# Four layers of attention and experts on one Trainium2 core: square roots and a sigmoid moved from ScalarE to VectorE

## The chip, the core and the metric

The kernel runs on one core of a Trainium2 chip. A core has five engines that run their own queues of instructions: TensorE (PE in the profile; PEld is its loading of weights), VectorE (DVE), ScalarE (ACT), GpSimd (POOL) and SyncE (SP). They meet in semaphores: an instruction waits in its queue until what it needs is there, and everything behind it in the queue waits too. ScalarE evaluates functions such as Exp, Silu or Sqrt from tables; before a function whose table is not the loaded one, its queue holds an ACT_TABLE_LOAD. Time is the device time of one execution in microseconds (us). The measured number is the median of several runs; one more run is recorded by the profiler and read in detail.

## What is computed

Activations `x` (4 sequences of 512 tokens, 256 features) pass through four layers. Each layer normalizes `x`, adds a cross attention to a context of 64 rows a sequence, normalizes again, and adds a feed-forward part:

```python
x = x + _L0_xattn_ref(_layernorm(x), ctx_1024, ...)     # softmax attention, 16 heads
x = x + _L0_ffn_ref(_layernorm(x), ...)                 # 8 experts, 2 for each token
x = x + _L1_xattn_ref(ctx_1024, ctx_1024, _layernorm(x), ...)  # exponential features
x = x + _L1_ffn_ref(_layernorm(x), ...)                 # latent attention, then 7 experts
x = x + _L2_xattn_ref(_layernorm(x), ctx_1024)          # nearest context row by cosine
x = x + _L2_ffn_ref(_layernorm(x), ...)                 # FP4 quantized feed-forward
x = x + _L3_xattn_ref(_layernorm(x), ctx_1024, ctx_1024, ...)
x = x + _L3_ffn_ref(_layernorm(x), ...)                 # 8 experts, 2 for each token
```

The change touches the roots and the sigmoid in these formulas:

```python
def _layernorm(x, axis=-1, eps=1e-05):
    m = jnp.mean(x, axis=axis, keepdims=True)
    v = jnp.var(x, axis=axis, keepdims=True)
    return (x - m) / jnp.sqrt(v + eps)
...
def rmsnorm(x, w):                                      # layer 1, twice
    norm = jnp.sqrt(jnp.mean(x * x, axis=-1, keepdims=True)) + EPS
    return x / norm * w
...
probs = jax.nn.sigmoid(logits)                          # layer 1, the router
...
def _l2norm(x):                                         # layer 2, tokens and context
    n = jnp.linalg.norm(x, axis=-1, keepdims=True)
    return x / jnp.maximum(n, EPS)
```

## The kernel before

The 2048 tokens lie in 16 tiles of 128 rows that stay in SBUF; four tiles (512 tokens, one sequence) are a group. Every stage is a loop over the four groups, written as Python generators whose steps are taken in turn, so that the next group's norm and queries fall between the current group's products. A framework then orders the instructions of each engine by its own estimate, except where the program fixes the order: on TensorE in the cross attentions and in the latent attention, on VectorE and SyncE in the three routed expert stages.

*Layer norm* (`layernorm_steps`, L336 to L345): four pairs of statistics on VectorE into `ln_mv`, a square root of four columns on ScalarE (`ln_sd`, L339), then on VectorE a reciprocal (`ln_rs`, L342) and the shift (`ln_sh`, L343), then four normalizations on ScalarE (`xn`, `xl` or `l2xn`, L345). Every stage begins with one for each group.

*Cross attentions* (layers 0, 1, 3; three stretches of the profile): the scores of a group come in two halves of four PSUM banks (`ps_cx`, L557 and L561) and there is one buffer for them. ScalarE's exponential (`cpr`, L563) must have read the first half before TensorE can write the second. The next group's norm and the routing norm of the group before are in ScalarE's queue in the same stretch. Then come the sums (`crs`, L581), the values (`ps_cy`, `ps_p`) and the residual addition (`x`, L615).

*Routed experts* (layers 0, 1, 3): blocks of 128 rows are fetched, transposed (`ps_xe`, `e_xT`), multiplied with the gate and up weights (`ps_gu`, L1044), passed through Silu on ScalarE (`e_s`, L1060) and a product on VectorE (`e_h`, L1061), transposed (`ps_he`, `e_hT`), multiplied with the down weights (`ps_de`, L1086), weighted (`e_y`, L1088) and scattered by GpSimd (L1089). The routing of the last group and the first results run between the blocks.

*Latent attention* (layer 1): `mla_heads` makes a layer norm (`xl`), an RMS norm (sum of squares on ScalarE at L354, square root `rms_n` at L362, `rms_e` at L364, `rms_r` at L366, scaling `xn` on VectorE at L368), and the heads. In the loop TensorE makes scores (`ps_ms`, L1283), VectorE takes the row maxima (`mq`, L1288), TensorE makes the transposed scores (`ps_mx`, L1298), ScalarE the exponential (`mpr`, L1300), GpSimd the mask (L1302), TensorE the sums (`ps_mo`, L1321). After each group a second RMS norm and the router follow (`mla_after`), with the sigmoid at L1380. Before its loop GpSimd clears the tiles of the heads (L1401 to L1408).

*Layer 2*: the context's norm (`l2_context`, L1519), then for each group a layer norm, a sum of squares and the length of each token (L1545 to L1548), the similarities (`ps_sim`, `sim` at L1557) and the chosen row; then another layer norm, and for each tile the FP4 quantization (`f_am` to `f_y`, L1584 to L1612 on VectorE, the last product on GpSimd, L1613), the products (`ps_f`, L1731), Silu (`fs`, L1741), the second quantization and the down product (`ps_fd`, L1753).

## Time and profile before

| what | us |
|---|---|
| median of 3 runs | 1979.29 |
| lowest and highest of them | 1974.59, 1983.53 |
| the profiled execution | 1971.78 |
| its span | 1970.1 |
| mean granted clock of TensorE in it | 0.933 |

| stretch of the span | what runs | span, us | TensorE busy | VectorE busy | ScalarE busy |
|---|---|---|---|---|---|
| 0 to 166 | cross attention 0 | 166 | 121.9 | 88.1 | 59.5 |
| 166 to 543 | experts 0 | 377 | 361.3 | 179.7 | 101.6 |
| 543 to 695 | cross attention 1 | 152 | 129.5 | 66.4 | 61.8 |
| 695 to 1175 | latent attention | 480 | 420.0 | 220.7 | 189.6 |
| 1175 to 1375 | experts 1, start of layer 2 | 200 | 163.7 | 109.9 | 74.7 |
| 1375 to 1560 | layer 2, FP4 | 185 | 166.7 | 158.3 | 85.5 |
| 1560 to 1700 | cross attention 3 | 140 | 110.2 | 77.9 | 50.7 |
| 1700 to 1970 | experts 3 and the end | 270 | 240.4 | 106.8 | 61.0 |

The busy times are those of the profile's stretches, added where two or three of them make one row. A row of a group of instructions is read like this: line, engine, operation, what it writes and reads, how many, then busy time and mean ns of one, then the idle time of the engine just before them and what ended it. The chain that ended last goes back from the last instruction to what released it at each step; a piece of it has its start, its length, and engine, tile and line. "Issue" is time in which the engine waited for nothing that the profile shows.

### The profile page before, as it was taken

Reading aid. Unit: us, or ns where it says so; the run is one execution under the profiler, and the core shown is the slowest. Engines: PE = TensorE matmul, PEld = TensorE weight load, DVE = VectorE, ACT = ScalarE, POOL = GpSimd, SP = SyncE. Lnnn points to the kernel's source line nnn. Section 1 sums busy time; section 2 is a strip of 40 time slices with the busy share of each in tenths; the row PEclk is TensorE's granted clock in tenths of the full one; section 3 lists DMA queues with packets and bytes.
Section 4 is the critical chain, followed back from the end, with each engine's and each line's share of the span. In section 5 each row is a group of like instructions: output and inputs, shape, how many; then the busy total and the mean of one; then the engine's idle time right before and its main releaser. Section 6 shows DMA issues by size and latency. Waiting matters only on the chain.

```text
span 1970.1 us, 25945 instructions
## 1 busy us (share of the span) xinstructions
PE 1713.7 (87%) x8752; PEld 972.3 (49%) x8752; DVE 1007.7 (51%) x2979; ACT 684.3 (35%) x1265; POOL 448.9 (23%) x626
## 2 busy tenths in 40 slices
PE   5878999999979878898999888887898887899995
PEld 2435666666645333343443344444565544455553
DVE  3655544445444444444455535546899556553332
ACT  3343222223244232335344433234455343322221
POOL 2031211123230021122122222233313102221133
PEclk7988999999979978998999998998999889899998
DMA  9629778878300000000002034873000001679885
GB/s 277 183 77 339 253 288 285 293 286 307 131 25 1 17 24 1 1 1 22 1 5 64 12 106 155 293 261 104 13 1 1 12 1 36 235 268 318 298 321 199
DMA packets 109349, 271.61 MB, mean 138 GB/s; under 512 B 13408, under 2 KB 71200, under 8 KB 99104
## 3 DMA queue, kind: packets, MB, share of 16 engines
q1 hardware_dynamic: 87648, 232.42, 35.0%
q0 software_dynamic: 10176, 28.00, 3.7%
q10 hardware_dynamic: 11392, 9.53, 1.5%
q8 instruction: 70, 1.15, 0.2%
q14 instruction: 63, 0.52, 0.1%
HBM read 220.48 MB, written 49.42 MB: 137 GB/s over the span
## 4 chain that ended last, share of the span: by engine, by line
PE 68%; DVE 17%; ACT 7%; issue 3%; POOL 2%; DMA 2%; ACTq 0%; SPq 0%; DVEq 0%; POOLq 0%
PE ps_gu L1044 20%; PE ps_de L1086 9%; PE ps_ms L1283 4%; PE ps_mo L1321 3%; PE ps_p L612 2%; DVE mq L1288 2%; PE ps_f L1731 2%; PE ps_mx L1298 2%; PE ps_bc L591 2%; PE ps_he L1073 2%; PE ps_xT L377 2%; ACT cpr L563 2%; PE ps_cx L557 1%; PE ps_cy L597 1%; ACT xn L345 1%
## 5 line engine op out<-in xcount | busy, mean ns | idle before, releaser
L1044 PE MATMUL ps_gu<-e_wgu,e_xT 128*128 128x352 f32 (+1 forms) x1088 | 429.3, 535 | 21.7 <-DVE e_xT L1036 14.6
L1044 PEld LDWEIGHTS ps_gu<-e_wgu,e_xT 128*128 128x128 f32 x1088 | 198.0, 193 | 164.2 <-issue 70.3
L1086 PE MATMUL ps_de<-e_wd,e_hT 128*128 128x256 f32 x932 | 239.0, 394 | 10.8 <-ACT e_hT L303 4.8
L1086 PEld LDWEIGHTS ps_de<-e_wd,e_hT 128*128 128x128 f32 x932 | 175.7, 194 | 84.5 <-issue 39.0
L1061 DVE TENSOR_TENSOR e_h<-e_s,ps_gu 128x352 f32<-128x352 f32 (+2 forms) x155 | 83.3, 537 | 253.5 <-PE ps_gu L1044 183.8
L1089 POOL DMA_INDIRECT ys<-e_y,e_to x116 | 114.1, 984 | 422.1 <-ACT e_y L1088 282.3
L1288 DVE TENSOR_REDUCE mq<-ps_ms 128x2 f32<-128x256 f32 (+3 forms) x128 | 105.7, 825 | 136.3 <-PE ps_ms L1286 136.1
L1060 ACT ACTIVATE e_s<-ps_gu 128x352 f32<-128x352 f32 (+2 forms) x155 | 74.1, 478 | 267.9 <-PE ps_gu L1044 261.7
L1088 ACT ACTIVATE e_y<-ps_de,e_wt 128x256 f32<-128x256 f32 x116 | 55.0, 474 | 258.2 <-PE ps_de L1086 251.0
L1300 ACT ACTIVATE mpr<-ps_mx 128x1024 f32<-128x1024 f32 (+3 forms) x128 | 90.1, 704 | 146.5 <-PE ps_mx L1298 143.6
L1283 PE MATMUL ps_ms<-mkT,mqT 32*128 32x512 f32 (+3 forms) x512 | 111.5, 514 | 23.6 <-DVE mq L1288 22.4
L873 POOL DMA_INDIRECT xs<-xn,e_at x96 | 94.6, 986 | 118.7 <-DVE e_fi L907 37.8
L1302 POOL TENSOR_SCALAR_AFFINE_SELECT mpr<-mpr 128x256 f32<-128x256 f32 x128 | 52.1, 410 | 245.1 <-ACT mpr L1300 245.0
L1298 PE MATMUL ps_mx<-mqm,mkT 32*128 32x128 f32 (+3 forms) x512 | 106.9, 494 | 0.9 <-ACT mpr L1300 0.9
L1321 PE MATMUL ps_mo<-mpr,va 128*32 128x128 f32 (+3 forms) x512 | 96.4, 458 | 4.5 <-POOL mpr L1302 4.5
L1073 PE MATMUL ps_he<-consts_sb,e_h 128*128 128x128 f32 x466 | 76.6, 277 | 16.4 <-DVE e_h L1061 13.7
L1167 POOL TENSOR_TENSOR x<-x,e_r 128x256 f32<-128x256 f32 x90 | 66.7, 751 | 84.5 <-DMA e_r<-ys 81.0
L1731 PE MATMUL ps_f<-w,xqT 128*128 128x352 f32 x256 | 84.5, 471 | 0.9 <-ACT xqT L1699 0.9
L557 PE MATMUL ps_cx<-q,kbd 32*128 32x512 f32 x256 | 45.8, 818 | 44.0 <-ACT cpr L563 44.0
L1283 PEld LDWEIGHTS ps_ms<-mkT,mqT 32*128 32x128 f32 x512 | 40.7, 194 | 78.7 <-DVE mq L1288 54.2
L1033 DVE COPY e_xT<-ps_xe 128x256 f32<-128x256 f32 x78 | 32.9, 422 | 80.6 <-PE ps_xe L1030 80.6
L1073 PEld LDWEIGHTS ps_he<-consts_sb,e_h 128*128 128x128 f32 x466 | 54.0, 139 | 38.7 <-DVE e_h L1061 23.7
(317 smaller groups left out, 2814.7 us busy)
## 6 DMA issues: line engine op xcount, KB each, us to landing
e_wgu<-in_e0gu SPq DMA_DIRECT2D x39, 1408.0 KB, 6.3
e_wgu<-in_e3gu SPq DMA_DIRECT2D x39, 1024.0 KB, 5.6
e_wd<-in_e0d SPq DMA_DIRECT2D x39, 768.0 KB, 5.9
e_wd<-in_e3d SPq DMA_DIRECT2D x39, 512.0 KB, 5.7
e_wgu<-in_e1gu SPq DMA_DIRECT2D x38, 512.0 KB, 4.2
xs<-z SPq DMA_DIRECT2D x16, 1040.0 KB, 15.0
e_x<-xs SPq DMA_DIRECT2D x116, 130.0 KB, 5.1
e_r<-ys SPq DMA_DIRECT2D x46, 256.0 KB, 3.9
```

The lines of the kernel that those rows point to most:

```text
L873: r = nc.gpsimd.indirect_dma_start(out=net.xs, out_offset=bass.IndirectOffsetOnAxis(ap=at[:, k, i : i + 1], axis=0), in_=rows[:, i], in_of ...
L1044: nc.tensor.matmul(ps[:, :n], xT[:, c], wgu[:, c, cols], start=(c == 0), stop=(c == NC - 1))
L1061: nc.vector.tensor_tensor(h[:, k * H : (k + 1) * H], s, u, ALU.mult)
L1073: self.nc.tensor.transpose(ps[:r, f - f0], h[:, f * P : f * P + r], net.ident)
L1086: nc.tensor.matmul(po[:, :E], hT[:r, f], wd[:r, f], start=(f == 0), stop=(f == self.nf - 1))
L1089: r = nc.gpsimd.indirect_dma_start(out=net.ys, out_offset=bass.IndirectOffsetOnAxis(ap=at, axis=0), in_=y, in_offset=None)
L1283: nc.tensor.matmul(ps[:, r, :n], st.qT[o][rows, diag], st.kT[o][rows, :n], start=True, stop=False)
L1288: nc.vector.tensor_reduce(st.q[:, i, at : at + 2, HD], ps[:, :, :n], AX.X, ALU.max, negate=True)
L1298: nc.tensor.matmul(ps[:, r, :n], st.kT[o][rows, keys], st.qm[o][rows, j * P :], start=True, stop=True)
L1300: nc.scalar.activation(pr[:, :, :n], ps[:, :, :n], AF.Exp, scale=HD**-0.5)
L1321: nc.tensor.matmul(st.po[32 * n : 32 * n + 32, j * P :], st.va[:, j, at : at + 32], pr[:, r, : S - j * P], start=(j == 0), stop=(j == GT - 1),
L1731: nc.tensor.matmul(ps[:, :H], xT[:, c], w[:, c, k * H : (k + 1) * H], start=(c == 0), stop=(c == NC - 1))
```

## The change

All roots go from ScalarE to VectorE. A function `one_over_root` takes a first guess from the bits of the number (an integer view times -0.5 plus a constant), computes the error `v*y*y - 1`, and multiplies the guess with a series of four terms in it: nine VectorE operations on 128x4 values, each of which needs the one before. The layer norm adds epsilon on VectorE and takes the result as its reciprocal root; the RMS norm multiplies the mean square with it to get the root, then goes on as before; the lengths of layer 2 are capped at 1e12 instead of having the root bounded below by 1e-12. The router's sigmoid becomes Exp on ScalarE, plus one and reciprocal on VectorE.

```diff
+ROOT = float(0x5F374800)
+SERIES = (-0.49999833, 0.37499796, -0.31393766, 0.27487816)
...
-        self.eps = c.tile([P, 1], F32, tag="eps", name="eps")
-        nc.vector.memset(self.eps, 1e-5)
...
+    def one_over_root(self, v):
+
+        vec, shape = self.nc.vector, list(v.shape)
+        y, t, e, p = (self.sm(f"rq_{n}{shape[1]}", [P, shape[1]])[: shape[0]] for n in "ytep")
+        vec.tensor_scalar(y.bitcast(I32), v.bitcast(I32), -0.5, ROOT, ALU.mult, ALU.add)
+        vec.tensor_tensor(t, v, y, ALU.mult)
+        vec.tensor_tensor(e, t, y, ALU.mult)
+        vec.tensor_scalar(e, e, -1.0, None, ALU.add)
+        c1, c2, c3, c4 = SERIES
+        vec.tensor_scalar(p, e, c4, c3, ALU.mult, ALU.add)
+        vec.tensor_tensor(p, p, e, ALU.mult)
+        vec.scalar_tensor_tensor(p, p, c2, e, ALU.add, ALU.mult)
+        vec.scalar_tensor_tensor(p, p, c1, e, ALU.add, ALU.mult)
+        vec.scalar_tensor_tensor(y, p, 1.0, y, ALU.add, ALU.mult)
+        return y
...
-        sd = self.sm("ln_sd", [P, GT])
-        nc.scalar.activation(sd, mv[:, :, 1], AF.Sqrt, bias=self.eps)
-        yield
-        rs, sh = self.sm("ln_rs", [P, GT]), self.sm("ln_sh", [P, GT])
-        nc.vector.reciprocal(rs, sd)
+        var = self.sm("ln_var", [P, GT])
+        nc.vector.tensor_scalar(var, mv[:, :, 1], 1e-5, None, ALU.add)
+        yield
+        rs, sh = self.one_over_root(var), self.sm("ln_sh", [P, GT])
...
-        nr = self.sm("rms_n", [P, GT])
-        nc.scalar.activation(nr, ss, AF.Sqrt, scale=1.0 / E)
+        ms = self.sm("rms_m", [P, GT])
+        nc.vector.tensor_scalar(ms, ss, 1.0 / E, None, ALU.mult)
         ne = self.sm("rms_e", [P, GT])
-        nc.vector.tensor_scalar(ne, nr, 1e-5, None, ALU.add)
+        nc.vector.tensor_tensor(ne, ms, self.one_over_root(ms), ALU.mult)
+        nc.vector.tensor_scalar(ne, ne, 1e-5, None, ALU.add)
...
-        nc.scalar.activation(pb, lg, AF.Sigmoid)
-        yield
+        nc.scalar.activation(pb, lg, AF.Exp, scale=-1.0)
+        yield
+        nc.vector.tensor_scalar(pb, pb, 1.0, None, ALU.add)
+        nc.vector.reciprocal(pb, pb)
         yield
...
+    def one_over_length(self, ss):
+
+        rs = self.one_over_root(ss)
+        self.nc.vector.tensor_scalar(rs, rs, 1e12, None, ALU.min)
+        return rs
...
-        l2, lm, lr = (self.sm(n, [P, GT]) for n in ("l2_n", "l2_m", "l2_r"))
-        nc.scalar.activation(l2, sq, AF.Sqrt)
-        yield
-        nc.vector.tensor_scalar(lm, l2, 1e-12, None, ALU.max)
-        nc.vector.reciprocal(lr, lm)
+        yield
+        lr = self.one_over_length(sq)
```

In `l2_context` the same three operations are replaced by `one_over_length(ss)`.

## The prediction

> **What bounds the kernel now.** I read first the busy times and the chain of work that ended last, then the groups by line on ScalarE, then the chain and the timeline at the places where norms stand, and last the stretches by stage.

> ```profile
> PE 1713.7 (87%) x8752; PEld 972.3 (49%) x8752; DVE 1007.7 (51%) x2979; ACT 684.3 (35%) x1265; POOL 448.9 (23%) x626
> PE 68%; DVE 17%; ACT 7%; issue 3%; POOL 2%; DMA 2%; ACTq 0%; SPq 0%; DVEq 0%; POOLq 0%
> L339 ACT ACT_TABLE_LOAD x25 | 32.1, 1283 | 14.1 <-DVE ln_mv L337 7.2 <-DMA ctxT<-in_ctxT 5.6 <-issue 0.9
> L563 ACT ACT_TABLE_LOAD x12 | 15.4, 1283 | 0.2
> ```
> TensorE is the bound on average and ScalarE is mostly idle, so table loads matter only where the chain runs through them. ScalarE's groups by line hold 103 loads of 1.283 us: 25 + 12 here, 17 + 14 + 10 at L1060, L1300 and L1741 (ahead of Silu and Exp), 25 in smaller groups. Adding up the chain's own pieces gives 32.4 us of them on the chain; the rest lie in idle time. A typical place, from the chain in the first cross attention:

> ```profile
> 99.99 1.28 ACT L339
> 101.29 0.31 ACT ln_sd L339
> 102.11 2.07 ACT xn L345 x4
> 104.20 1.28 ACT L563
> 105.50 1.89 ACT cpr L563
> 107.42 2.09 PE ps_cx L557 x8
> ```
> The square root's table is loaded, the norm follows, Exp's table comes back, and only then can the softmax exponential (cpr) free the one score buffer TensorE waits for. The reader is to see both switches in series. The timeline of VectorE prices the replacement:

> ```profile
> 158.13 0.17 DVE L908 CAST e_full<-e_fi 128x8 f32<-128x8 int32 x1
> 158.33 0.19 DVE L909 TENSOR_TENSOR e_till<-e_till,e_full 128x32 f32<-128x32 f32 x1
> 158.56 0.18 DVE L910 TENSOR_TENSOR e_count<-e_till 128x24 f32<-128x24 f32 x1
> 158.77 0.18 DVE L911 TENSOR_TENSOR e_count<-e_count,e_taken 128x24 f32<-128x24 f32 x1
> ...
> 911.35 0.19 DVE L726 TENSOR_TENSOR t_eq<-t_rest,t_m 128x28 f32<-128x28 f32 x1
> 911.46 0.16 DVE L772 TENSOR_TENSOR t_s<-t_m 128x4 f32<-128x4 f32 x1
> 911.57 0.19 DVE L729 SCALAR_TENSOR_TENSOR t_at<-t_eq,consts_sb 128x28 f32<-128x28 f32 x1
> ```
> Small operations that need each other start 0.21 us apart; with another's between them, 0.11 us. Last, where VectorE has no room (the expert-free FFN with FP4) and where GpSimd is in its way (the start of the latent attention):

> ```profile
> 1375.00:1560.00 185.00, 166.67 (x691) 110.65 (x691) 158.33 (x390) 85.50 (x181) 49.48 (x53) 0.97 0.02 7
> ...
> 699.52 1.01 DVE L364 TENSOR_SCALAR rms_e<-rms_n 128x4 f32<-128x4 f32 x1
> 700.78 4.32 DVE L368 TENSOR_SCALAR xn<-xl,rms_r 128x256 f32<-128x256 f32 x4
> ...
> 697.67 0.95 POOL L1401 MEMSET mq<- 128x1024 f32 x1 [55.70 <-PE ps_p L612]
> ```
> In the first line the third busy time is VectorE's, 158.33 of 185 us; the chain there runs for 82 us through VectorE. In the others, while GpSimd clears tiles, a 128x4 operation takes 1.01 us (median of this line 0.17) and a scaling 1.08 (median 0.35).

> **The change, part by part.** The built order of the changed program holds 26 table loads, so 77 go, with 45 square roots (32 of 0.30 us, 13 of 0.21): 77 x 1.283 + 12.3 = 111 us of ScalarE. What stays is Exp against Silu. VectorE gets 423 instructions more, 423 x 0.11 to 0.21 = 47 to 89 us. TensorE and the DMA queues keep their instructions (SP's order is the same), so what counts is the path. A layer norm's tail on VectorE (variance plus epsilon, nine operations, shift) is 11 x 0.21 = 2.3 us; before, square root, reciprocal and shift without a load took 101.99 - 101.29 = 0.7. So each norm on the path loses 1.6 us and wins 1.28 for each load that stood in series. By stage:

> *Cross attention 0 (0 to 166 us).* Group 2, shown above: the last statistics end at 99.91; the shift was ready at 101.99, now at 99.91 + 2.3 = 102.2; Exp's load of 1.28 goes: -1.0. Group 1 (exponential at 72.08): two norms stand ahead, and in the new order the exponential waits for five of eight normalizations instead of seven; the second chain ends near 70.0, the exponential starts near 70.6: -1.5. Group 3: VectorE's chain is woven into the routing table, about +0.8, one normalization moves behind the exponential (-0.5), the load goes: -1.1. Start: the second group's chain (11 operations among statistics) delays a transposed copy at 19.46 by some 0.5. Together -3.1 (bounds -6 and 0).

> *Experts 0.* No load is on the chain. The ten operations stand in one piece in VectorE's fixed order, ahead of an e_h that moves from 178.36 to about 179.4; TensorE has the down products until 181.0, so 0; without that cover +1.0.

> *Cross attention 1.* Between the two exponentials of group 0 (562.52 and 572.05) lie two loads and three square roots. Statistics were ready by 559.3, so the norms are done when ScalarE turns to them, eight normalizations end at 568.5, TensorE has the scores at 569.0: -3.0. In groups 1 to 3 the load before the exponential (602.01, 635.42, 667.96) goes, but scores come only at 602.8: -0.5 each. Together -4.5 (bounds -6 and -2).

> *Latent attention, start.* 22 small operations now stand between 698.5 and the scaling at 700.78, while GpSimd clears tiles. If eight of them each wait out a clearing (1.0 us), the scaling starts at 707, and then runs undisturbed, 1.14 for four as at 708.50: it ends at 708 against 705.1. If none waits it starts at 701, as before. I take +2.5 (0 to +4).

> *Latent attention, loop.* Five lumps of 11 to 24 operations stand in VectorE's queue ahead of the row maxima (mq) for which TensorE waits; a lump of 13 is 2.6 us, VectorE idles about 1.6 us in a step of 3, so about 0.8 to 1 each: +4; the load on the chain at 895.91 goes, -1.3. Together +2.7 (bounds -1.3, no lump felt, and +9.7, all five at 2.2).

> *Experts 1 and the tail.* The RMS norm at 1182.75 has 13 operations, 2.7 us, for a load, a root and two operations, 1.9: +0.8. The sigmoid: its load and Silu's after it stay (both are in the new order), two operations more: +0.4. The context's norm at 1229.58: -0.5 (0 to -2.8, since VectorE's lump of ten takes the place of ScalarE's two loads ahead of e_h). Layer norms at 1320.8 and 1348: +1.6 each, less a load each: +0.7. At 1363.10, 1367.36 and 1368.88 loads of 3.6 go with nothing in their place, because the new chain is needed only at sim: -3.6. Together -2.2 (bounds -8 and +4).

> *FP4 stage.* Three groups x 26 operations = 78, woven between long ones: 78 x 0.11 = 8.6, of which I count 80%, since norms stand where the chain is VectorE's: 6.9. GpSimd adds 2 (the nearest row, f_sc, means 0.274 where undisturbed ones of this size take 0.17: 0.1 each, for about 20). The load at 1397.17 goes. Together +7.6 (bounds 0 and +15.1, which is 78 x 0.21 less the load).

> *Cross attention 3 and experts 3.* Three places like those of cross attention 0 (1606.98, 1640.27, 1672.79): -3.6. At 1709.50 the norm stood ahead of Silu's second half on ScalarE (Silu at 1712.88); in the new order it stands behind, and e_h starts when VectorE's lump ends, 1711.2 for 1713.51: -2.3.

> *The clock.* After the waits of 3.88 and 3.79 us at 107.42 and 1643.49 eight score products took 2.09 us, against 1.14 at 63.39: half clock. A wait shorter by 1.0 may escape it; products and the eight that follow would win 1.5 each. I take -1.5 for both (0 to -3).

> Sum: -3.1 + 0 - 4.5 + 2.5 + 2.7 - 2.2 + 7.6 - 3.6 - 2.3 - 1.5 = **-4.4 us**. The profiled execution took 1971.78 (span 1970.1, 1.7 around it), so it would take 1967.4. The median of the runs shown, 1979.29, lies 7.5 higher; with that, 1974.9.

> [...] At 70.79 a load of 1.28 us is followed by its exponential at 72.08, so the row gives a switch 1.29 us. [...]

> **Rivals.** (1) *VectorE's new work is hidden.* For it: VectorE is 51% busy, and most of the 78 have long neighbours. Against it: windows of 10.00 in 10 us at 1445 to 1465. With +1 in place of +7.6 and +1.5 in place of the latent attention's +5.2, the sum is -14.7: 1964.6. (2) *VectorE becomes the bound*: in the FP4 stage and in the latent attention operations cost their full dependent spacing, +15.1, +4 and +9.7 in place of +7.6, +2.5 and +2.7, with the clock as it was: +13.1, 1992.4. It decides once these three stages together lose more than 25 us, since all the others win 15.7 without the clock. For it: the 82 us of chain on VectorE; against it: the weaving in the new order. (3) *The loads that go were nearly all hidden and the norms' longer tail pays back the others*: every stage within 1 us, 1979. Against it the six pairs like the one shown.

> **How the numbers follow.** Forecast 40%, rival 1 29%, rival 2 26%, rival 3 5%. About 0.5% (9.9 us) is what a measurement of this kernel can tell from no change. The forecast and rival 3 lie within it: 45%; rival 1 is faster, 29%; rival 2 slower, 26%. The predicted time is the forecast's, 1975; its own range, 1966 to 1985. The whole range reaches most of the way into both rivals, 1960 to 1995.

> **What would show it.** About 26 loads of 1.28 us on ScalarE and none beside a norm; the wait of ps_cx for cpr (44.0 us on TensorE over 12 waits) down by 8 to 12; VectorE busy 50 to 85 us more; the stretch of the FP4 stage longer by about 8 us, cross attentions shorter by 3 to 5 each; the scaling at L368 of group 0 starting 2 to 6 us after the last residual add. The forecast is wrong if FP4 and latent attention together lose under 2 or over 25 us.

## The result and the profile after

| | before | changed |
|---|---|---|
| median, us | 1976.33 (20 runs) | 1977.52 (20 runs) |
| lowest, highest | 1973.9, 1983.53 | 1966.96, 1983.76 |
| profiled execution, its span | 1971.78, 1970.1 | 1972.83, 1971.0 |

The ratio changed to before is 0.9998, its 95% interval 0.9986 to 1.0011: no difference that can be measured. The lines of the changed kernel lie 18 below those of before (Silu's L1060 is L1078, the score exponential's L563 is L581, the normalization's L345 is L362); the new root is L332 to L341. First its busy times and the chain that ended last, from the page:

```profile
PE 1708.8 (87%) x8752; PEld 968.9 (49%) x8752; DVE 1063.7 (54%) x3402; ACT 574.5 (29%) x1143; POOL 447.8 (23%) x626
PE 69%; DVE 18%; ACT 4%; issue 3%; DMA 2%; POOL 2%; another core or an unknown queue 1%; SPq 0%; ACTq 0%; DVEq 0%; POOLq 0%
```

ScalarE lost 109.8 us (684.3 to 574.5), VectorE won 56.0 us and 423 instructions, and ScalarE's share of the chain fell from 7% to 4%. The whole of this is worth nothing at the end of the program. Two groups of table loads on ScalarE, and then TensorE's waits (us in total, times, longest):

```profile
L1078 ACT ACT_TABLE_LOAD x7 | 9.0, 1283 | 15.5 <-PE ps_gu L1062 6.8 <-DVE e_tab L980 5.3 <-DVE e_row L971 3.4
L581 ACT ACT_TABLE_LOAD x1 | 1.3, 1283 | 0.0
```

```profile
PE ps_cx L575 <- ACT cpr L581: 34.4, 10, 7.1
PE ps_ms L1301 <- DVE mq L1306: 22.9, 42, 1.7
```

Of 17 loads ahead of Silu 7 are left, of twelve ahead of the score exponential one, and TensorE's wait for it fell from 44.0 to 34.4 us. The second line is the wait for the row maxima of the latent attention; before, the same view had:

```profile
PE ps_ms L1283 <- DVE mq L1288: 22.4, 41, 1.3
```

The place that the prediction showed first, group 2 of cross attention 0, in the changed kernel's timelines of VectorE, ScalarE and TensorE (start, length, engine):

```profile
97.33 0.17 DVE L357 TENSOR_SCALAR ln_var<-ln_mv 128x4 f32<-128x4 f32 x1
...
99.33 0.16 DVE L360 SCALAR_TENSOR_TENSOR ln_sh<-ln_mv,rq_y 128x4 f32<-128x4 f32 x1
...
99.61 2.07 ACT L362 ACTIVATE xn<-x,ln_sh,rq_y 128x256 f32<-128x256 f32 x4 [6.10 <-DVE ln_sh L360]
101.59 1.85 ACT L581 ACTIVATE cpr<-ps_cx 128x2048 f32<-128x2048 f32 x1
...
103.49 1.14 PE L575 MATMUL ps_cx<-q,kbd 32*128 32x512 f32 x8 [2.57 <-ACT cpr L581]
```

The last statistics end at 97.30 and the shift at 99.49: a tail of 2.19 us, eleven operations 0.20 apart. The four normalizations follow, then the exponential at once, with no load between. TensorE waits 2.57 us where it waited 3.88, and its eight score products take 1.14 us at a granted clock of 1.00, where they took 2.09 at 0.50 (half clock). TensorE's timeline of before had:

```profile
107.42 2.09 PE L557 MATMUL ps_cx<-q,kbd 32*128 32x512 f32 x8 [3.88 <-ACT cpr L563]
```

The time by stage comes from the start of each matrix product: a stretch runs from one product to another, the same two in every kernel, and is named by its times in the first profile of before. Both kernels were profiled a second time (the first and the fifth run below), so each has two lengths.

| stretch | what runs | predicted | before, us | changed, us | difference of the means |
|---|---|---|---|---|---|
| 0 to 166 | cross attention 0 | -3.1 and half of the clock's -1.5 | 165.2, 164.6 | 161.3, 159.3 | -4.6 |
| 166 to 470 | experts 0 | 0 | 304.8, 304.7 | 305.4, 304.9 | +0.4 |
| 470 to 540 | end of experts 0 | 0 | 70.1, 69.9 | 75.9, 75.4 | +5.6 |
| 540 to 672 | cross attention 1 | -4.5 | 132.0, 131.3 | 126.3, 126.2 | -5.4 |
| 672 to 716 | latent attention, start | +2.5 | 43.7, 43.7 | 45.2, 45.3 | +1.6 |
| 716 to 1180 | its loop | +2.7 | 464.1, 463.8 | 474.0, 474.0 | +10.1 |
| 1180 to 1376 | experts 1 and the tail | -2.2 | 196.1, 194.2 | 194.3, 193.9 | -1.1 |
| 1376 to 1560 | FP4 stage | +7.6 | 184.0, 189.9 | 188.5, 188.7 | +1.7 |
| 1560 to 1706 | cross attention 3 | -3.6 and half of the clock's -1.5 | 145.9, 143.4 | 135.3, 135.2 | -9.4 |
| 1706 to the last product | experts 3 | -2.3 | 244.5, 244.4 | 245.2, 245.2 | +0.8 |

So 20 us are won in four stretches (three cross attentions and the tail) and given back in the others. The clock has a hand in the two largest rows, as the stretches of the span show (length, busy times of TensorE, its weight loads, VectorE, ScalarE, GpSimd, then the mean granted clock). The latent loop and cross attention 3 of before:

```profile
715.84:1179.94 464.10, 411.28 (x2521) 182.86 (x2520) 209.71 (x477) 179.82 (x307) 103.56 (x207) 0.94 0.07 21
1560.00:1705.93 145.93, 114.92 (x772) 60.73 (x772) 82.55 (x261) 51.72 (x68) 27.27 (x32) 0.84 0.19 63
```

and of the changed kernel:

```profile
714.10:1188.08 473.98, 419.01 (x2520) 184.85 (x2520) 222.87 (x554) 160.06 (x289) 103.52 (x206) 0.92 0.06 21
1570.89:1706.14 135.25, 106.00 (x772) 56.28 (x772) 85.95 (x297) 42.11 (x58) 27.20 (x32) 0.92 0.20 68
```

The same products kept TensorE busy 7.7 us longer in the loop, at clock 0.92 for 0.94, and 8.9 us shorter in cross attention 3, at 0.92 for 0.84.

### The profile page after: what moved, and what is told of

Read it like the earlier page. It is cut to its first block, busy times and chain, and to the rows that moved or that the text cites. A ratio compares the mean times of both kernels' runs of the same rounds, so it can differ in the third digit from the quotient of the medians.

```text
span 1971.0 us, 26231 instructions
## 1 busy us (share of the span) xinstructions
PE 1708.8 (87%) x8752; PEld 968.9 (49%) x8752; DVE 1063.7 (54%) x3402; ACT 574.5 (29%) x1143; POOL 447.8 (23%) x626
## 4 chain that ended last, share of the span: by engine, by line
PE 69%; DVE 18%; ACT 4%; issue 3%; DMA 2%; POOL 2%; another core or an unknown queue 1%; SPq 0%; ACTq 0%; DVEq 0%; POOLq 0%
PE ps_gu L1062 20%; PE ps_de L1104 10%; PE ps_ms L1301 4%; PE ps_mo L1339 3%; DVE mq L1306 2%; PE ps_p L630 2%; PE ps_mx L1316 2%; PE ps_f L1749 2%; PE ps_he L1091 2%; PE ps_fd L1771 2%; PE ps_bc L609 2%; PE ps_cs L544 1%; PE ps_ms L1304 1%; PE ps_cx L575 1%; DVE mx L552 1%
## 5 line engine op out<-in xcount | busy, mean ns | idle before, releaser
L1104 PE MATMUL ps_de<-e_wd,e_hT 128*128 128x256 f32 x932 | 236.6, 391 | 13.1 <-ACT e_hT L305 5.2
L1306 DVE TENSOR_REDUCE mq<-ps_ms 128x2 f32<-128x256 f32 (+3 forms) x128 | 105.6, 825 | 137.5 <-PE ps_ms L1304 134.0
L1078 ACT ACTIVATE e_s<-ps_gu 128x352 f32<-128x352 f32 (+2 forms) x155 | 73.9, 477 | 294.4 <-PE ps_gu L1062 275.6
L1301 PE MATMUL ps_ms<-mkT,mqT 32*128 32x512 f32 (+3 forms) x512 | 113.1, 520 | 24.4 <-DVE mq L1306 22.9
L1091 PE MATMUL ps_he<-consts_sb,e_h 128*128 128x128 f32 x466 | 77.4, 279 | 12.6 <-DVE e_h L1079 7.1
L1091 PEld LDWEIGHTS ps_he<-consts_sb,e_h 128*128 128x128 f32 x466 | 54.3, 139 | 34.1 <-DVE e_h L1079 15.7
L575 PE MATMUL ps_cx<-q,kbd 32*128 32x512 f32 x256 | 41.1, 739 | 34.6 <-ACT cpr L581 34.4
```

The source lines that it names most:

```text
L1091: self.nc.tensor.transpose(ps[:r, f - f0], h[:, f * P : f * P + r], net.ident)
L1104: nc.tensor.matmul(po[:, :E], hT[:r, f], wd[:r, f], start=(f == 0), stop=(f == self.nf - 1))
L1301: nc.tensor.matmul(ps[:, r, :n], st.qT[o][rows, diag], st.kT[o][rows, :n], start=True, stop=False)
L1306: nc.vector.tensor_reduce(st.q[:, i, at : at + 2, HD], ps[:, :, :n], AX.X, ALU.max, negate=True)
```

## The experiments

Ratios are to runs of before on the same chip; its medians there were 1977.0 (runs 1 to 4), 1972.0 (5 to 8), 1971.0 (9 to 12) and 1974.6 (13), so times of different groups are not compared, only ratios. A ratio is an estimate with its own interval and can differ from the quotient of the two medians by up to 0.0015 (run 13: 0.9951, and 0.9936 by the medians); differences between runs that are smaller than this are not read. Run 4, which put one power operation of VectorE in place of the nine, gave no time and shows nothing.

| run | what it is | median, us | ratio | 95% interval |
|---|---|---|---|---|
| 1 | changed kernel again | 1976.62 | 0.9999 | 0.9985 to 1.0014 |
| 2 | series in eleven norms ahead of a cross attention | 1979.48 | 1.0008 | 0.9995 to 1.0022 |
| 3 | series in all but these | 1979.68 | 1.0010 | 0.9995 to 1.0025 |
| 5 | before again | 1970.87 (one run) | | |
| 6 | series in both norms of the cross-attention stages | 1965.12 | 0.9965 | 0.9952 to 0.9977 |
| 7 | series in all but these | 1980.77 | 1.0044 | 1.0027 to 1.0060 |
| 8 | changed kernel, two terms | 1964.91 | 0.9967 | 0.9950 to 0.9984 |
| 9 | square root in the norm inside experts 0 | 1965.59 | 0.9965 | 0.9952 to 0.9978 |
| 10 | GpSimd's additions apart from that norm | 1976.74 | 1.0030 | 1.0020 to 1.0040 |
| 11 | square root in the latent attention | 1966.38 | 0.9967 | 0.9955 to 0.9980 |
| 12 | run 6 with two terms | 1959.05 | 0.9930 | 0.9917 to 0.9943 |
| 13 | two terms, square root in both places of runs 9 and 11 | 1961.96 | 0.9951 | 0.9933 to 0.9968 |

Most runs put ScalarE's square root back at some places. For this the layer norm got a flag, and each caller says which it wants:

```
-    def layernorm_steps(self, g, out):
+    def layernorm_steps(self, g, out, series=False):
...
+        if series:
             var = self.sm("ln_var", [P, GT])
...
             rs, sh = self.one_over_root(var), self.sm("ln_sh", [P, GT])
+        else:
+            sd = self.sm("ln_var", [P, GT])
+            nc.scalar.activation(sd, mv[:, :, 1], AF.Sqrt, bias=self.eps)
+            yield
+            rs, sh = self.sm("rq_y4", [P, GT]), self.sm("ln_sh", [P, GT])
+            nc.vector.reciprocal(rs, sd)
```

**1. The changed kernel again.** No edit.

> The changed kernel once more, unedited. Comparing the start of each matrix product in the first profiled executions of the two kernels gave, changed minus before: cross attention 0 -3.4 us; experts 0 +5.4 in one jump at 470 to 474; cross attention 1 -4.6; latent attention's start +1.5 and its loop +9.3 (jumps at 894, 1040 and 1110); tail -1.8; FP4 stage +4.5; cross attention 3 -10.7; experts 3 +1.4; together +1. Theory: gains and losses belong to the program, so each of these stages comes back within 1.5 us and the time is within 0.3% of before. Rival: the jumps are chance of one execution; then several stages differ by 4 us or more from the first profile.

Every stretch came back within 0.6 us, but for cross attention 0 (159.3 for 161.3). By these two profiles the gains and losses belong to the program; run 5 shows how far two profiles of one program can differ.

**2 and 3. One norm of each cross attention, and the rest.** In run 2 the norm ahead of the attention asks for the series, all others take the square root; in run 3 it is the other way round. `fine` is set for layer 1's first norm alone.

```
# run 2
-        for _ in self.layernorm_steps(st.g, xn):
+        for _ in self.layernorm_steps(st.g, xn, series=not fine):
# run 3, with series=True as the default
+        for _ in self.layernorm_steps(st.g, xn, series=fine):
```

> The series on VectorE only in the layer norms of the twelve cross-attention groups but one (layer 1's first, which is normed while experts 0 run); there and everywhere else the square root and the sigmoid on ScalarE as before. Theory (the loads that went pay in the cross attentions, the series costs elsewhere): -3.4 - 4.6 - 10.7, so about -18 us against before, 1958 (1954 to 1965). Rival (the loads were mostly hidden, and the stages' differences come from the order of the whole program or by chance): within 5 us of before.

> The opposite division: ScalarE's square root in those eleven cross-attention norms, the series and the sigmoid from an exponential in everything else. Theory: +5.4 + 10.8 - 1.8 + 4.5 + 1.4, so about +18 to +20 us against before, 1995 (1988 to 2000). Rival: within 5 us of before. If the two halves don't add up to the whole (0 us) within 5 us, the edits act on each other.

The theory's -18 and +18 fell, and in number the rival came true: the two halves are equal to before within 0.25%, less than 5 us. The cut was a bad one, since a group of cross attentions 0 and 3 has a second norm, ahead of the routing, and run 2 left its square root there (Exp and the square root still alternate). TensorE's waits for the exponential tell this without the clock. At the two later places of these stages they are 3.88 and 8.40 us (cross attention 0) and 3.79 and 8.33 (cross attention 3) in before, the same within 0.02 in run 2, but 2.57, 7.09, 2.52 and 7.02 in run 3, as in the changed kernel. At the first place of each stage run 3 leaves 5.01 and 4.45 us, before has 4.99 and 4.94, and the changed kernel, with the series in both norms, 3.68 and 3.55. So most of the gain sits with the routing's norms, and the first place needs both norms for its full gain. Run 2 taught a second thing. Its latent attention has no series in it, and yet it lost 1.65 us at one wait for the row maxima, with half clock behind it (four products take 3.72 us for 1.94). TensorE's timeline of run 2:

```profile
1042.16 1.14 PE L1309 MATMUL ps_ms<-mkT,mqT 32*128 32x384 f32 x4 [1.65 <-DVE mq L1314]
...
1045.29 3.72 PE L816 MATMUL ps_sg<-xnT,sgu 128*128 128x512 f32 x4
```

The same products in run 7, where this stage does have the series:

```profile
1047.61 0.59 PE L1310 MATMUL ps_ms<-mkT,mqT 32*128 32x384 f32 x2
...
1048.59 1.94 PE L817 MATMUL ps_sg<-xnT,sgu 128*128 128x512 f32 x4
```

This wait, with 4.2 us lost behind it in run 2, stands in the profiles of the changed kernel (both), of run 3, and of runs 2 and 13, which have the square root there; runs 7 to 10, which have the series, are without it. So the longer chain isn't what makes it. In the changed kernel's profile VectorE (1041.73) and ScalarE (1041.74) both resume 0.6 us after the same products of TensorE end; why they wait for those was not found.

**5. Before again.** No edit.

The clock theory, against the old one of runs 1 to 3 that sums the stages of two profiles, was formed on the profiles of runs 1 to 3.

> The kernel before once more, unedited. New theory: TensorE's clock is granted in stretches that are multiples of 3.41 us, laid from a start that is another one in each execution; a wait that falls on such a stretch costs up to 1.7 us per stretch after it, and most of the stage differences between the first two profiles are that (TensorE busy at half clock, before against changed: cross attention 3 34.9 and 14.7 us, latent loop 47.0 and 63.4). Then this profile differs from the first one of the same program by over 3 us in at least two stages, and stage length less half of TensorE's busy time at half clock agrees within 2 us. Rival: the stages' lengths belong to the program: all within 1.5 us of the first profile.

Neither expectation held. One stretch differs by over 3 us, not two (FP4: 184.0 and 189.9; cross attention 3: 145.9 and 143.4), so the clock theory's first number failed, and so did the rival's 1.5 us. In the FP4 stage the clock does account for most of it: TensorE was busy for 9.9 and 20.0 us at half clock, and half of that difference is about 5 of the 5.9. The clock theory's second number failed as well: length less half of the half-clock time differs by 4.1 us in cross attention 0 (146.2 and 150.3). A single profile's stage is uncertain by some 2 us, and the FP4 stage by 6.

**6 and 7. Both norms of the cross-attention stages, and the rest.** As runs 2 and 3, with the routing's norm on the same side:

```
             xn = rows[:, :, :E]
-            yield from self.layernorm_steps(g, xn)
+            yield from self.layernorm_steps(g, xn, True)
```

> The second run's division widened: the series on VectorE in both norms of the cross-attention stages (ahead of the attention and ahead of the routing, all but layer 1's first), ScalarE's square root and sigmoid in everything else, so that only the loads of those stages go. By the stage sum of the first two profiles (old theory): -3.4 - 4.6 - 10.7, 1958. By the clock theory the stages' gain at full clock is 0.2 - 2.2 - 0.6: within 0.3% of before, 1971 to 1981.

> The complement: square root on ScalarE in both norms of the cross-attention stages, series and exponential in everything else. Old theory: +18 us, 1995. Clock theory: what the changed kernel lost at full clock outside the cross attentions, experts 0 +3.3, latent loop +1.7, tail +2.6, FP4 +1.8, together +9, 1986 (1980 to 1990).

Cut at the right place the parts tell themselves apart: -0.35% and +0.44%, or -6.9 and +8.7 us. Together +0.09%, and the whole has -0.02%: they add up. The old theory's 18 is too large for both. The clock theory's loss, +9, was right; its -2.6 was under the gain. In cross attention 1 the norm that shares ScalarE's queue with the exponential is the latent attention's, which run 6 leaves on the square root: TensorE's last three waits there, 0.54, 0.61 and 2.53 us in before, are still 0.54, 0.61 and 2.52 in run 6, and 0.08, 0.08 and 2.00 in run 7 and in the changed kernel.

**8. A shorter series.** Two terms in place of four, six operations for nine.

```
-        vec.tensor_scalar(e, e, -1.0, None, ALU.add)
-        c1, c2, c3, c4 = SERIES
-        vec.tensor_scalar(p, e, c4, c3, ALU.mult, ALU.add)
+        vec.tensor_scalar(p, e, 0.37592661, -1.25294482, ALU.mult, ALU.add)
         vec.tensor_tensor(p, p, e, ALU.mult)
-        vec.scalar_tensor_tensor(p, p, c2, e, ALU.add, ALU.mult)
-        vec.scalar_tensor_tensor(p, p, c1, e, ALU.add, ALU.mult)
-        vec.scalar_tensor_tensor(y, p, 1.0, y, ALU.add, ALU.mult)
+        vec.scalar_tensor_tensor(y, p, 1.87701824, y, ALU.add, ALU.mult)
```

> The changed kernel with a series of two terms in place of four: six operations in place of nine for each root (its error is 2.5e-5 instead of 2e-8: two terms are left out). 96 VectorE operations less, at 0.11 to 0.21 us 10 to 20 us of VectorE. If the chain's length is what the change pays outside the cross attentions: a third of +9, so -3, and up to -0.6 for each of the 12 cross-attention groups: 5 to 9 us below the changed kernel. If the length is mostly covered: within 2 us of it.

0.9967: 6.5 us below before and about 6 below the changed kernel, within the first theory's 5 to 9. A shorter series pays, but its profile does not show the whole gain on the chain. TensorE's six waits for the exponential in cross attentions 0 and 3 are shorter by 0.1 to 0.6 us each, 2.0 together, and the end of experts 0 fell from 75.6 to 72.8. The largest difference is the latent loop, 461.8 us for 474.0, and there TensorE was busy at half clock for 37.0 us instead of 63.4: half of that is 13.2.

**9 and 10. The norm inside experts 0.** Run 9 gives this norm alone the square root (`series=not fine`, all others the series). Run 10 keeps the series and takes GpSimd's work out of its way:

```
                         for _ in self.ctx_normed(made, R_FCB, fine=True):
-                            next(results, None)
                             yield
                         yield from results
```

> The changed kernel with ScalarE's square root kept in one norm alone, layer 1's first, which stands in VectorE's fixed order while experts 0 run. Three profiles with the series there (changed, changed again, the rest) had 75.9, 75.4 and 75.9 us for the stretch 470 to 540, four with the square root 69.9 to 70.3. If this loss reaches the end: 5.5 us less than the changed kernel and than before, ratio 0.9972, and the stretch back at 70. Rival: a later wait takes it up; within 2 us of the changed kernel.

> The changed kernel, but the generator that adds expert results to x on GpSimd no longer takes a step between the steps of that one norm; it goes on behind it. If GpSimd's additions make the chain dear (its 128x4 operations took 0.54 to 0.69 us in place of 0.17), these go back to 0.16 to 0.21 us, the lump of ten falls from 5.0 to 2.2 us and the stretch 470 to 540 from 75.5 to about 72.5: 2 to 3 us less than the changed kernel. Rival (the lump's length in VectorE's order alone, or what stands ahead of it): the operations stay dear, or the stretch stays at 75.

Run 9 won 5.4 to 6.9 us (0.9965, against 0.9998 to 1 for the changed kernel), all that its stretch had lost (70.3 for 75.6). What makes it dear is seen in the changed kernel's timelines of VectorE, GpSimd and TensorE:

```profile
469.67 0.58 DVE L334 TENSOR_TENSOR rq_e<-rq_t,rq_y 128x4 f32<-128x4 f32 x1
470.28 0.66 DVE L335 TENSOR_SCALAR rq_e<-rq_e 128x4 f32<-128x4 f32 x1
...
473.23 0.57 DVE L360 SCALAR_TENSOR_TENSOR ln_sh<-ln_mv,rq_y 128x4 f32<-128x4 f32 x1
473.73 0.41 DVE L1051 COPY e_xT<-ps_xe 128x256 f32<-128x256 f32 x1
...
468.50 3.23 POOL L1185 TENSOR_TENSOR x<-x,e_r 128x256 f32<-128x256 f32 x4 [7.46 <-DMA e_r<-ys]
...
474.19 6.69 PE L1062 MATMUL ps_gu<-e_wgu,e_xT 128*128 128x352 f32 x16 [2.71 <-DVE e_xT L1051]
```

and in run 10's timelines of VectorE and TensorE:

```profile
468.08 0.17 DVE L335 TENSOR_SCALAR rq_e<-rq_e 128x4 f32<-128x4 f32 x1
...
469.28 0.16 DVE L360 SCALAR_TENSOR_TENSOR ln_sh<-ln_mv,rq_y 128x4 f32<-128x4 f32 x1
469.36 0.42 DVE L1051 COPY e_xT<-ps_xe 128x256 f32<-128x256 f32 x1
...
469.83 5.00 PE L1062 MATMUL ps_gu<-e_wgu,e_xT 128*128 128x352 f32 x16
```

While GpSimd adds, an operation of VectorE on 128x4 takes up to 0.69 us (the first of the ten); without it, nine of the ten take 0.16 or 0.17 (the tenth, beside GpSimd's product of the quantization, 0.47). With the copy in time, TensorE has no wait of 2.71 us ahead of the sixteen gate products, and they take 5.00 us for 6.69: 4.4 us. The stretch fell from 75.6 to 71.4, more than the 2 to 3 expected. That part is shown. And yet the whole program of run 10 is slower, 1.0030. Its profile has cross attention 1 as in the changed kernel, and then loses 5.3 us in experts 1, where nothing was edited. TensorE's timeline of the changed kernel there:

```profile
1195.00 1.14 PE L395 MATMUL ps_xT<-consts_sb,xn 128*128 128x128 f32 x8 [1.49 <-DVE xn L386]
...
1198.62 1.96 PE L1062 MATMUL ps_gu<-e_wgu,e_xT 128*128 128x512 f32 x4
...
1201.01 1.11 PE L1104 MATMUL ps_de<-e_wd,e_hT 128*128 128x256 f32 x4
```

and of run 10:

```profile
1190.53 1.13 PE L395 MATMUL ps_xT<-consts_sb,xn 128*128 128x128 f32 x8 [1.49 <-DVE xn L386]
...
1194.89 3.76 PE L1062 MATMUL ps_gu<-e_wgu,e_xT 128*128 128x512 f32 x4
...
1199.58 2.05 PE L1104 MATMUL ps_de<-e_wd,e_hT 128*128 128x256 f32 x4
```

The same instructions, after the same wait of 1.49 us, 4.5 us earlier in the run: but the four gate products take 3.76 us for 1.96, half clock, and of the lead of 4.5 us 0.3 is left at the next down products (1203.28 and 1203.00). This profile is one execution; that all ten timed runs lost their lead at this place isn't shown. But all ten ran at a lower granted clock, 0.927 to 0.932, than the fifteen runs of before on the same chip (0.934 to 0.940), and in the profile TensorE was busy at half clock for 225.4 us, the most of all profiles (184.5 and 175.8 in the changed kernel's two). So run 10 loses by the clock in every run; which of its waits the clock falls behind, and why in this program, stays open.

**11. The latent attention.** The square root back in its layer norms and RMS norms, the series elsewhere.

> The changed kernel with ScalarE's square root kept in the latent attention alone (its layer norms and both RMS norms, 12 norms). By the profiles its loop is 474.0 us with the series and 464 before, its start 45.2 against 43.7: if that belongs to the series, 10 to 11 us less than the changed kernel, ratio to before 0.9945. Rival by the halves' times: experts 0 and the rest without the latent attention already make up 5.5 + 3 of the 8.8 that the complement lost, so 1 to 3 us less; the loop's half-clock stretches then come back elsewhere.

0.9967, so 6.5 us by the ratio and 4.7 by the medians: between the two expectations. Its loop took 463.3 us, 10.7 less, as the first one said, but a part didn't reach the end. The stretch of the loop in run 11:

```profile
717.18:1180.49 463.31, 409.61 (x2522) 182.51 (x2520) 211.41 (x483) 171.99 (x301) 103.18 (x207) 0.94 0.06 21
```

VectorE has 11.5 us less to do in it than in the changed kernel, TensorE 9.4 us less, at clock 0.94 for 0.92, with the same products. Taking all profiles together: six with the four-term series in this loop took 472.1 us on the mean, seven with the square root 465.7. TensorE's busy time at half clock was 61.9 and 47.9 us in them; half of the difference, 7.0, is more than the 6.4 between the lengths. The wait for the row maxima, 22.9 us in the changed kernel, is 22.4 in before and 23.3 in run 11. So in the profiles the loop pays in half clock, and not in row maxima that wait behind lumps of small operations. Run 8 says the same: with two-term series in the loop it had the least half clock of all, 37.0 us, and the shortest loop, 461.8, below all seven with the square root. Length less half of the half-clock time is 441.2 with the series, 441.7 with the square root and 443.3 in run 8. Why the four-term series brings more half clock here, no run shows.

**12 and 13. Versions that should beat both.** Run 12 is run 6 with two terms; run 13 has two terms everywhere but in the norm of run 9 and the latent attention of run 11.

> The version that should beat both: the series only in the two norms of the cross-attention stages, with two terms instead of four (its error 2.5e-5; two terms are left out), square root and sigmoid on ScalarE elsewhere. 6.9 us below before without the shortening; three operations fewer on the path at 0.21 in each of some ten places and their share of the 6.5 that the shortening gave in the whole kernel (a third to a half): 9 to 10 us below before, ratio 0.995 (0.993 to 0.9965). Rival: the chain is covered in these stages, so the same 0.9965 as without the shortening.

> Each place by what the runs gave: ScalarE's square root in layer 1's first norm and in the latent attention, the series everywhere else (cross attentions, the L2 attention, FP4 stage), with two terms instead of four (error 2.5e-5; two terms are left out), sigmoid from an exponential. If the parts add up: the changed kernel (0) less 6.9 for the one norm, less 6.5 for the latent attention and less a share of the 6.5 to 6.9 for the shortening: -16 to -20 us against before, ratio 0.991 (0.990 to 0.992). If the parts overlap, since the one norm and the latent attention each gave back what the same later waits took: -12, ratio 0.994, no better than the twelfth version.

Run 12 has the lowest ratio of all: 1959.05 us against 1971.03, 0.9930, twice what run 6 won and more than the 9 to 10 us expected; why more, no run tells. Run 13 should have been faster still if gains of places added up, and is not shown to be: 0.9951 by the ratio, and by the medians level with run 12 (0.9936 and 0.9939). Of the 16 to 20 us that its parts promised, 9.7 came by the ratio, 12.6 by the medians. Its latent loop, with the square root, took 468.6 us and has a wait of 1.4 us at the place shown for run 2. So gains of different places don't simply add up here, and no run tells why; a shift of where later waits meet the clock would do it, but that is not shown.

## Why the prediction was right, and where it was not

The forecast was no change, 1975 us; 1977.52 was measured, and there was no change. That the time is within 2.5 us is luck, in two ways. The sum, -4.4 us, did not come (the ratio is 0.9998), and it had been added to a median of three runs, 1979.29, which lies 3.0 above that of twenty. And the terms of the sum missed by far more than the sum: the cross attentions, the FP4 stage and the start of the latent attention came out 13.5 us better than forecast, the two stretches of experts 0, the latent loop, experts 3 and the tail 17.6 us worse. The forecast's own ground, that gains in the cross attentions are paid back elsewhere, was right. Where they are paid back was half wrong: in the latent loop, but by another step than the one named, hardly in the FP4 stage, and in experts 0, which was put at 0.

**Right.** The cross attentions, in sign and mechanism: -12.7 with the clock's share, -19.4 measured (-4.6, -5.4 and -9.4). The tail of 2.3 us for 2.19; the load that stood in series; the wait shorter by 1.0 (1.31 measured): the place above shows all three. The six waits of this kind in cross attentions 0 and 3 fell by 1.27 to 1.39 us each, 7.9 together, for the 7.2 that the working gave these six places; the changed kernel's second profile has the same six waits within 0.02 us. That such a product then escapes half clock is not sure: the wait at the place above was 2.57 or 2.58 us in seven profiles, and its eight products took 1.14 us in four of them, 1.56, 2.09 and 2.09 in the other three. The wait for the exponential fell by 9.6 in all (8 to 12 were named), 26 loads stayed, at 1.283 us each, VectorE won 56.0 (50 to 85). The latent attention's start, +2.5, came as +1.6; its scaling began 3.2 us later when the lead of 1.7 that it had up to there is added (700.78 and 702.25), and then ran with little in its way, 1.62 us for 4.32.

The prediction gave a switch the 1.29 us of a row. At the place it showed first the rows of before agree: the normalization ends at 104.18, the load runs from 104.20 to 105.48 and the exponential starts at 105.50, 1.30 us after the load's start.

**Too small.** Cross attention 3, -3.6 and half of -1.5 against -9.4. Six profiles with the series in both its norms took 137.5 us on the mean, three with the square root 143.9; of these 6.4 the half clock's share is 3.6 (21.5 for 28.6 us at half clock), and 2.8 remain, close to the 3.6 of the working. So the term that was mis-sized is the clock: I gave two places 1.5 together. Where it falls is chance in part: the six profiles lie between 135.2 and 140.9 us, with 14.6 to 29.6 us at half clock, and the two behind the -9.4 are the two shortest.

**Wrong.** *Experts 0*, "the ten operations stand in one piece ... TensorE has the down products until 181.0, so 0". I worked it out at the first norm of the stage and not at the one at its end, where GpSimd adds expert results to x at the same time: an operation takes up to 0.69 us for 0.17, the copy for the next expert (e_xT) is late, and products behind it run at half clock (7.4 us of TensorE's busy time in this stretch on the mean of the two profiles, 3.1 before). +5.6; run 9 shows that it is this norm, run 10 that GpSimd's additions make 4.2 of it. I had seen this blocking at 699.52 (1.01 us) and had put it into the latent attention and the FP4 stage, where it cost little.

*The latent loop*, "five lumps ... about 0.8 to 1 each: +4". The wait that was to grow didn't (22.4 and 22.9). The loop lost 10.1 in the profiles, and 6.4 on the mean, by half clock behind waits, one of which has nothing to do with the series. Right sign, wrong step; why the series brings the half clock stays open.

*The FP4 stage*, "78 x 0.11 = 8.6, of which I count 80%". Seven profiles with the four-term series took 188.6 us on the mean, five with the square root 187.6: +1.0. The chain runs through VectorE for 82 us there, but the stage grew by less than an eighth of the 8.6 us, so the added operations mostly found room. Rival 1 was right about this stage, and rival 2's ground, that VectorE becomes the bound, fell with it.

*Experts 3*, -2.3. The start won 0.7 (e_h comes 1.9 us earlier there, but TensorE's products only 0.7). In the built order two down products have moved ahead of the gate products near the end (1925) and wait 1.0 us for VectorE's copy; that costs 1.4.

Rival 3 (nearly all hidden, every stage within 1 us) gave the right time, 1979, for a wrong reason: eight of ten stretches moved by more than 1 us.

## What to carry to other kernels

In this kernel, where ScalarE's loads of 1.28 us stood in series with an exponential that frees a buffer, the longer dependent chain on VectorE paid (the six waits in cross attentions 0 and 3 fell by 1.27 to 1.39 us each); where the same norm stands in VectorE's fixed order beside GpSimd's additions, it didn't (+5.6 us). So change such a helper by call site, not everywhere: the change as made is worth nothing, the same series at the right sites and with no more terms than are needed is worth 0.7% (run 12, interval 0.6 to 0.8%). And when two stages are compared by profile, profile both kernels twice and take TensorE's half-clock time beside the lengths, or a wait like run 2's, 1.65 us with 4.2 lost behind it, will be read as the program's own.

## What the hardware showed

Beside GpSimd's work some small operations of VectorE took three to six times as long. In the norm inside experts 0 of the changed kernel, beside six additions of 0.72 to 0.91 us and a product of 0.61 on GpSimd, seven of the ten 128x4 operations took 0.54 to 0.69 us and three 0.16 or 0.17; in run 10, without the additions, nine of the ten took 0.16 or 0.17. Of the seven, five have two inputs and two have one (L332, 0.69 us; L335, 0.66). At the start of the latent attention GpSimd clears tiles, and its rows there (MEMSET, 0.95 to 1.09 us for a large tile) name no input: there seven operations with one input, of 128x4, took 0.53 to 0.99 us, and all fourteen with two inputs 0.15 or 0.16. Why operations with two inputs took longer in the first place and not in the second, no run shows.
